# A two-layer image kernel: softplus arithmetic and part of the B-products move to GpSimd, and the state tiles shrink to one state

## The chip, the cores and the metric

The kernel runs on one core of one Trainium2 chip. The metric is the device time of one execution in microseconds: 26,680.71 us is the median of three runs before the change (26,676.87 to 26,696.96). The profile shows one further execution on the same core. Engines are named as in the profile: PE is the matrix engine, DVE the vector engine, ACT the activation engine, POOL is GpSimd, SP issues most of the transfers.

## The reference, cut to what matters

The input is an image batch of 4 x 128 x 128 x 128 floats. Layer 0 is a deformable convolution (a gather of sampled points, weighted and summed, with a residual). Layer 1 is a two-deep Mamba block over the rows of the picture: each row is a sequence of 128 steps with 256 inner channels and 16 states. The change touches layer 1 alone:

```python
def _selective_scan(u, delta, A, Bm, Cm, Dp):
    deltaA  = exp(einsum('btd,dn->btdn', delta, A))
    deltaBu = einsum('btd,btn->btdn', delta * u, Bm)
    def step(h, xs):
        dA, dBu, c = xs
        h = dA * h + dBu
        return h, einsum('bdn,bn->bd', h, c)
    ...
    return y + u * Dp

dt, Bm, Cm = split(u @ xw)
delta = softplus(dt @ dtw + dtb)
```

So each channel and each of 16 states needs a product of delta\*u with B, a recurrence along the sequence, and a product of its result with C, summed over the states.

## The kernel before

**Tiling.** Layer 1 is cut into blocks of SR = 4 rows of 128 points (TB = 512 points), with the 256 channels as NC = 2 halves of 128 partitions. One *job* is one block in one of the two Mamba layers. There are 32 blocks in a picture and 4 pictures, so 64 jobs for each picture and 256 in all. `jobs` takes two blocks at a time, so that two independent jobs alternate.

**What a job does.** `pre` makes u (convolution by matmul and Silu), the gate g, the rows of B and C (written to DRAM as `bcd`), and delta = softplus(pdt). Softplus is written as max(x,0) + ln(1+e^-|x|), with a correction e: ACT makes |x| (L538), e^-|x| (L539), w1 = 1+e (L545) and ln w1 (L546); DVE forms w1-1-e (L547), max(x,0) minus that (L548), the sum with the logarithm (L549) and du = delta\*u (L550). `main` then walks the 16 states in 8 steps of NQ = 2 states. In each step SP loads B and C broadcast to all partitions (L570), ACT writes zero into the first column of each sequence of `da` (L575, so that the recurrence begins anew there) and exp(delta\*A) into the rest (L580), and DVE makes hs = du\*B once per state (L586, 128x1024), the recurrence in place in `da` for both states at once (L592, 128x2048), and the product with C in place, both states at once (L596, 128x2048). PE sums the transposed result over the states in PSUM (L128). At the end DVE multiplies by the gate (L607), whose first operand is in PSUM.

**Order.** `layer1` calls `pre` for job i+1 before `main` for job i, so softplus of the next job is made while this job's states run. `layer1` of picture b is interleaved with `layer0` of picture b+1 by a loop that steps both. The pictures thus overlap: first layer 0 of picture 0 alone, then three pictures' worth of both layers together, then layer 1 of the last picture alone. In layer 0 every unit issues 8 indirect gathers from POOL (L364), which read their indices from SBUF, and multiplies what they brought with weights on DVE (L382). The order within an engine is set by a scheduler at build time[...].

**Buffers.** `da` has three fixed buffers of two states, `hs` has one buffer, B and C have two buffers each, `e` two half-width ones, `w1` one.

Of the kernel before, what the change touches and what calls it, by code (L numbers as in the profile page):

```python
# [10 lines left out]
F32 = mybir.dt.float32  # L11
# [52 lines left out]
def block_kernel(ctx: ExitStack, tc: tile.TileContext, a: dict, out: bass.AP):  # L64
# [68 lines left out]


    dw = loadw("dw", [P, NT, NT], pool=p2, tag="dbl")
    dwb = loadw("dwb", [P, NT], pool=p2, tag="ot")
    pw = loadw("pw", [P, NT, CG], pool=p2, tag="u")
    pwb = loadw("pwb", [P, 1], pool=p2, tag="w1")
    nc.vector.tensor_tensor(
# [15 lines left out]
    alog = loadw("alog", [P, NL, NC, NS], pool=p2, tag="dbl")  # L155
    nc.scalar.activation(aneg, alog, AF.Exp)
    nc.vector.tensor_scalar(aneg, aneg, -1.0, None, ALU.mult)
    dpar = loadw("dpar", [P, NL, NC], pool=p2, tag="ot")
    for l in range(NL):
        for c in range(NC):  # L160
            nc.vector.tensor_scalar(ddiag[:, l, c, :], ident, dpar[:, l, c : c + 1], None, ALU.mult)
    inw = loadw("inw", [P, NL, NC * P], a["inw"][:, :, 0 : NC * P], pool=p2, tag="yg")
    cvw = loadw("cvw", [P, NL, DCONV, NC * P], pool=p2, tag="hs")
    for l in range(NL):
        nc.vector.tensor_tensor(
            inc[:, l], cvw[:, l], inw[:, l].unsqueeze(1).to_broadcast([P, DCONV, NC * P]), ALU.mult
        )


# [289 lines left out]

    NDA = 3
    das = [cw.tile([P, NC, NQ, SR, P], F32, name=f"da{i}") for i in range(NDA)]
    zero = cw.tile([P, NC * NQ * SR], F32, name="zero")
    nc.vector.memset(zero, 0.0)
    n_da = [0]

    NH = 2
# [15 lines left out]
    def pre(st, l):  # L484

        blk = st["blk"]
        nm = f"{blk}_{l}"
        if l == 0:
            x1t = load_x1(blk, nm)
            st["h"] = next_h()  # L490
            scale, bias = gn2[blk * SR // H]
            nc.scalar.activation(
                st["h"][:, :, DCONV - 1 :], x1t.rearrange("p (s t) -> p s t", s=SR),
                AF.Identity, scale=scale, bias=bias,
            )
        h = st["h"]
        u = p2.tile([P, NC, TB], F32, tag="u", name=f"u_{nm}")
        for c in range(NC):
            px = ps1.tile([P, TB], F32, tag="t", name=f"pu_{nm}_{c}")
            for j in range(DCONV):  # L500
                nc.tensor.matmul(  # L501
                    px.rearrange("p (s t) -> p s t", s=SR),
                    inc[:, l, j, c * P : (c + 1) * P],
                    h[:, :, j : j + P],
                    start=(j == 0),
                    stop=(j == DCONV - 1),
                )
            nc.scalar.activation(u[:, c], px, AF.Silu, bias=cvb[:, l, c : c + 1])  # L508
        g = p2.tile([P, SR, NC * P], F32, tag="g", name=f"g_{nm}", bufs=2)
        for i in range(SR // 2):  # L510
            px = ps1.tile([P, 2, NC * P], F32, tag="t", name=f"pr_{nm}_{i}")
            for j in range(2):
                nc.tensor.matmul(
                    px[:, j], h[:, 2 * i + j, DCONV - 1 :], resw[:, l, :],
                    start=(j == 0), stop=True, skip_group_check=True,
                )

            tc.keep_in_program_order(nc.scalar.activation(g[:, 2 * i : 2 * i + 2], px, AF.Silu))
        pdb = ps1.tile([P, TB], F32, tag="t", name=f"pdb_{nm}")
        for c in range(NC):  # L520
            nc.tensor.matmul(pdb[0:XP], xpw[:, l, c, :], u[:, c], start=(c == 0), stop=(c == NC - 1))  # L521

        dbl = p2.tile([XP, TB], F32, tag="dbl", name=f"dbl_{nm}")
        nc.scalar.activation(dbl, pdb[0:XP], AF.Identity, bias=xpb)  # L524
        bcd = pd.tile([2 * NS, TB], F32, tag="bcd", name=f"bcd_{nm}")
        nc.sync.dma_start(bcd, dbl[DTR + 1 : XP, :])


        de = p2.tile([P, NC, TB], F32, tag="de", name=f"de_{nm}", bufs=2)
        du = p2.tile([P, NC, TB], F32, tag="du", name=f"du_{nm}", bufs=2)  # L530
        es, pdts = [], []
        for c in range(NC):
            pdt = ps1.tile([P, TB], F32, tag="t", name=f"pdt_{nm}_{c}")
            nc.tensor.matmul(
                pdt, dtw[:, l, c * P : (c + 1) * P], dbl[0 : DTR + 1, :], start=True, stop=True
            )
            e = p2.tile([P, TB], F32, tag="e", name=f"e_{nm}_{c}", bufs=2)
            nc.scalar.activation(e, pdt, AF.Abs)  # L538
            nc.scalar.activation(e, e, AF.Exp, scale=-1.0)  # L539
            es.append(e)  # L540
            pdts.append(pdt)
        for c in range(NC):
            e = es[c]
            w1 = p2.tile([P, TB], F32, tag="w1", name=f"w1_{nm}_{c}")
            nc.scalar.activation(w1, e, AF.Identity, bias=1.0)  # L545
            nc.scalar.activation(du[:, c], w1, AF.Ln)  # L546
            nc.vector.scalar_tensor_tensor(e, w1, 1.0, e, op0=ALU.subtract, op1=ALU.subtract)  # L547
            nc.vector.scalar_tensor_tensor(de[:, c], pdts[c], 0.0, e, op0=ALU.max, op1=ALU.subtract)  # L548
        nc.vector.tensor_tensor(de, de, du, ALU.add)  # L549
        nc.vector.tensor_tensor(du, de, u, ALU.mult)  # L550
        st.update(u=u, g=g, delta=de, du=du, bcd=bcd)

    def main(st, l):

        blk = st["blk"]
        nm = f"{blk}_{l}"

        y = psy.tile([P, SR, NC, P], F32, tag="y", name=f"y_{nm}")
        for i in range(SR):
            for c in range(NC):  # L560
# [1 line left out]
                    y[:, i, c], st["u"][:, c, i * P : (i + 1) * P], ddiag[:, l, c, :],  # L562
                    start=(i % 2 == 0 and c == 0), stop=False, skip_group_check=True,
                )
        for q in range(NS // NQ):
            bc = []
            for w in range(2):
                t = p2.tile([P, NQ, TB], F32, tag=f"bc{w}", name=f"bc{w}_{nm}_{q}", bufs=2)
                n0 = w * NS + q * NQ
                nc.sync.dma_start(t, st["bcd"][n0 : n0 + NQ, :].partition_broadcast(P))  # L570
                bc.append(t)
            da = das[n_da[0] % NDA]
            n_da[0] += 1

            nc.scalar.copy(da.rearrange("p c n s t -> p (c n s) t")[:, :, 0], zero)  # L575
            for c in range(NC):
                dv = st["delta"][:, c].rearrange("p (s t) -> p s t", s=SR)
                for n in range(NQ):
                    s = q * NQ + n
                    nc.scalar.activation(  # L580
                        da[:, c, n, :, 1:], dv[:, :, 1:], AF.Exp, scale=aneg[:, l, c, s : s + 1]
                    )
            hs = p2.tile([P, NC, NQ, TB], F32, tag="hs", name=f"hs_{nm}_{q}")

            for n in range(NQ):
                nc.vector.scalar_tensor_tensor(  # L586
                    hs[:, :, n, :], st["du"], ones[:, 0:1],
                    bc[0][:, n].unsqueeze(1).to_broadcast([P, NC, TB]),
                    op0=ALU.mult, op1=ALU.mult,
                )  # L590
            df = da.rearrange("p c n s t -> p (c n s t)")
            nc.vector.tensor_tensor_scan(  # L592
                df, df, hs.rearrange("p c n t -> p (c n t)"), zero[:, 0:1], ALU.mult, ALU.add
            )
            dc = da.rearrange("p c n s t -> p c (n s t)")
            nc.vector.scalar_tensor_tensor(  # L596
                dc, dc, ones[:, 0:1],
                bc[1].rearrange("p n t -> p (n t)").unsqueeze(1).to_broadcast([P, NC, NQ * TB]),
                op0=ALU.mult, op1=ALU.mult,
            )  # L600
            for c in range(NC):
                for n in range(NQ):
                    for i in range(SR):
                        add_transposed(y[:, i, c], da[:, c, n, i, :], False, q == NS // NQ - 1 and n == NQ - 1)
            yield
        gt = st["g"]
        nc.vector.tensor_tensor(gt, y.rearrange("p s c d -> p s (c d)"), gt, ALU.mult)  # L607
        yg = p2.tile([P, NC, TB], F32, tag="yg", name=f"yg_{nm}")
# [6 lines left out]
        if l < NL - 1:  # L615
            for c in range(NC):
                nc.tensor.matmul(po, ow[:, l, c, :], yg[:, c], start=(c == 0), stop=(c == NC - 1))
            st["h"] = next_h()
            nc.scalar.copy(st["h"][:, :, DCONV - 1 :], po.rearrange("p (s t) -> p s t", s=SR))
        else:  # L620
            x1t = load_x1(blk, f"o{nm}")
            for i in range(SR):
                o = po[:, i * P : (i + 1) * P]
                nc.tensor.matmul(o, x1t[:, i * P : (i + 1) * P], ident, start=True, stop=False)
                for c in range(NC):
                    nc.tensor.matmul(
                        o, yg[:, c, i * P : (i + 1) * P], ow[:, l, c, :], start=False, stop=(c == NC - 1)
                    )
            ot = p2.tile([P, SR, P], F32, tag="ot", name=f"ot_{nm}")
            nc.scalar.copy(ot.rearrange("p r c -> p (r c)"), po)  # L630
            b, row = divmod(blk * SR, H)
            nc.sync.dma_start(out[b, row : row + SR].rearrange("r w c -> w r c"), ot)
# [115 lines left out]
```

## Time and profile before

| | |
|---|---|
| median of 3 runs | 26,680.71 us |
| the profiled execution | 26,698.06 us |
| its span | 26,696.0 us |
| DVE busy | 23,505.8 us (88%), 14,042 instructions |
| PE busy | 19,620.5 us (73%) |
| POOL busy | 16,017.0 us (60%), 9,216 gathers |
| ACT busy | 11,605.1 us (43%) |
| first recurrence (L592) starts | 3,471.2 us |
| POOL's last gather starts | 21,045.0 us |
| mean granted clock of PE | 0.845 |

The profiled execution lies 17 us above the median, 2 us of it outside its span. The busy shares of the whole span are averages over three stages: until about 3,471 us there is only layer 0; until about 21,100 us both layers run together; after it only layer 1 of the last picture is left, and POOL has nothing to do. A group's row gives the busy time of all its instructions and the mean of one; instructions of DVE that follow each other overlap by about 0.08 us in the records, so start-to-start distances in the timeline are a little smaller than the durations.

### The profile page before, as it was taken

To read this page: it belongs to the slowest core of one execution; us is meant where nothing else is said; L and a number is where in the kernel's file an instruction comes from. 1 tells how busy PE (TensorE), PEld (TensorE's weight loads), DVE (VectorE), ACT (ScalarE), POOL (GpSimd) and SP (SyncE) were. 2 spreads that over 40 slices of the span, in tenths; PEclk is the share of its full clock that TensorE was granted. 3 is DMA by queue.
4 is the path that set the end of the run, shared out by engine and by line. 5 is a ranking of instruction groups with operands and counts; after the bars stand their busy time and mean duration, and the time that the engine had idled before them with its cause. 6 is when DMAs were issued, how large, how long until landed. Compare 5 with 4: busy or idle time off the path is not lost. (4 is left out here: it accounts for less than half of the span.)

```text
span 26696.0 us, 294801 instructions
## 1 busy us (share of the span) xinstructions
PE 19620.5 (73%) x112196; PEld 13523.4 (51%) x112196; DVE 23505.8 (88%) x14042; ACT 11605.1 (43%) x18181; POOL 16017.0 (60%) x9222
## 2 busy tenths in 40 slices
PE   4777788878888778887888778888888655555555
PEld 3444455555555555555555555555555443434344
DVE  2232289999999999999999999999999999999999
ACT  0000044444444544444444454444445455555554
POOL 4777777878877767888878667877878400000000
PEclk7888888888999888888998888899998866666666
DMA  5363344456544444455544444444444333333332
GB/s 146 114 172 107 106 147 155 157 170 183 165 153 154 149 144 155 158 173 181 164 154 153 148 143 151 156 150 152 154 154 156 130 107 106 107 106 107 107 106 102
DMA packets 1994602, 3804.53 MB, mean 143 GB/s; under 512 B 771796, under 2 KB 1116116, under 8 KB 1993053
## 3 DMA queue, kind: packets, MB, share of 16 engines
q1 hardware_dynamic: 1550812, 2577.13, 29.9%
q0 software_dynamic: 442368, 1208.55, 14.4%
q8 instruction: 880, 14.42, 0.2%
q14 instruction: 542, 4.43, 0.0%
HBM read 3567.63 MB, written 217.05 MB: 142 GB/s over the span
## 5 line engine op out<-in xcount | busy, mean ns | idle before, releaser
L364 POOL DMA_INDIRECT gt<-table,idx x9216 | 16016.3, 1738 | 5031.5 <-issue 2999.5
L592 DVE TENSOR_TENSOR_SCAN da<-da,zero,hs 128x2048 f32<-128x2048 f32 x2048 | 9176.1, 4481 | 351.7 <-ACT da L580 247.1
L128 PE MATMUL y<-ident,da 128*128 128x128 f32 x32768 | 5252.0, 326 | 3956.1 <-DVE da L596 3955.4
L580 ACT ACTIVATE da<-de,aneg 128x508 f32<-128x508 f32 x8192 | 5550.5, 712 | 5605.2 <-PE y L128 5351.0
L128 PEld LDWEIGHTS y<-ident,da 128*128 128x128 f32 x32768 | 4682.4, 171 | 4953.3 <-DVE da L596 2520.6
L415 PE MATMUL acc<-s,wc 128*64 128x256 f32 (+3 forms) x38400 | 6403.2, 453 | 761.4 <-ACT s L396 760.9
L586 DVE SCALAR_TENSOR_TENSOR hs<-du,ones,bc 128x1024 f32<-128x1024 f32 x4096 | 5093.2, 1277 | 0.0
L415 PEld LDWEIGHTS acc<-s,wc 128*64 128x64 f32 x38400 | 3352.0, 145 | 3083.2 <-issue 1446.2
L596 DVE SCALAR_TENSOR_TENSOR da<-da,ones,bc 128x2048 f32<-128x2048 f32 x2048 | 4807.9, 2348 | 25.9
L382 DVE TENSOR_TENSOR gw<-gt,wt 128x1024 f32<-128x1024 f32 x2304 | 2786.4, 1213 | 2133.3 <-DMA gt<-table,idx 1500.9
L128 PE MATMUL p<-ident,gw 128*128 128x128 f32 x18432 | 2724.3, 299 | 1714.1 <-DVE gw L382 1706.7
L128 PEld LDWEIGHTS p<-ident,gw 128*128 128x128 f32 x18432 | 2292.8, 154 | 2329.3 <-DVE gw L382 1752.7
L396 ACT COPY s<-p 128x512 f32<-128x512 f32 x1152 | 668.6, 581 | 3989.8 <-PE p L128 3982.0
L501 PE MATMUL pu<-hp,inc 128*128 128x512 f32 x4096 | 1808.3, 593 | 0.0
L580 ACT ACT_TABLE_LOAD x1016 | 1303.5, 1283 | 16.8 <-PE y L128 5.7
L501 PEld LDWEIGHTS pu<-hp,inc 128*128 128x128 f32 x4096 | 751.2, 188 | 865.9 <-issue 865.2
L508 ACT ACTIVATE u<-pu,w_cvb 128x512 f32<-128x512 f32 x512 | 324.6, 684 | 1468.9 <-PE y L561 1461.4
L561 PEld LDWEIGHTS y<-ddiag,u 128*128 128x128 f32 x4096 | 579.5, 200 | 192.0 <-issue 192.0
L612 PE MATMUL pyg<-ident,g 128*128 128x128 f32 x2048 | 353.9, 328 | 425.7 <-DVE g L607 424.8
L546 ACT ACT_TABLE_LOAD x500 | 641.5, 1283 | 8.9
L561 PE MATMUL y<-ddiag,u 128*128 128x128 f32 x4096 | 612.1, 284 | 0.0
L263 PE MATMUL pof<-xn,w_offw 128*64 128x512 f32 x2304 | 585.0, 613 | 20.0 <-ACT xn L257 12.0
(118 smaller groups left out, 11036.3 us busy)
## 6 DMA issues: line engine op xcount, KB each, us to landing
bc<-bcd SPq DMA_DIRECT2D x4096, 512.0 KB
gt<-table,idx POOLq DMA_INDIRECT x9216
table<-xt SPq DMA_DIRECT2D x984, 128.0 KB
xt<-in_x SPq DMA_DIRECT2D x124, 320.0 KB
xr<-in_x SPq DMA_DIRECT2D x128, 256.0 KB
x<-xo SPq DMA_DIRECT2D x128, 256.0 KB
x1t<-x SPq DMA_DIRECT2D x128, 256.0 KB
x1t_o<-x SPq DMA_DIRECT2D x128, 256.0 KB
```

What stands on the lines that cost most here:

```text
L128: nc.tensor.matmul(o, v, ident, is_transpose=True, start=start, stop=stop, skip_group_check=True)
L364: nc.gpsimd.indirect_dma_start(out=gt[:, v, r], out_offset=None, in_=flat, in_offset=bass.IndirectOffsetOnAxis(ap=idx[:, ri, o : o + 1], a ...
L382: nc.vector.tensor_tensor(gw.rearrange("p r s v c -> p (r s) v c"), gts[h].rearrange("p v r (s c) -> p (r s) v c", c=CG), wv.unsqueeze(3). ...
L396: nc.scalar.copy(st[:, :, 1 : W + 1], p4)
L415: nc.tensor.matmul(accs[b, j + i0][CG * g : CG * g + CG, q : q + rb - ra, :], wc[sl, v, e, :], st[p + 4 * g if p < 4 else 8][sl, ra:rb, kx ...
L501: nc.tensor.matmul(px.rearrange("p (s t) -> p s t", s=SR), inc[:, l, j, c * P : (c + 1) * P], h[:, :, j : j + P], start=(j == 0), stop=(j ...
L546: nc.scalar.activation(du[:, c], w1, AF.Ln)
L561: nc.tensor.matmul(y[:, i, c], st["u"][:, c, i * P : (i + 1) * P], ddiag[:, l, c, :], start=(i % 2 == 0 and c == 0), stop=False, skip_grou ...
L580: nc.scalar.activation(da[:, c, n, :, 1:], dv[:, :, 1:], AF.Exp, scale=aneg[:, l, c, s : s + 1])
L586: nc.vector.scalar_tensor_tensor(hs[:, :, n, :], st["du"], ones[:, 0:1], bc[0][:, n].unsqueeze(1).to_broadcast([P, NC, TB]), op0=ALU.mult, ...
L592: nc.vector.tensor_tensor_scan(df, df, hs.rearrange("p c n t -> p (c n t)"), zero[:, 0:1], ALU.mult, ALU.add)
L596: nc.vector.scalar_tensor_tensor(dc, dc, ones[:, 0:1], bc[1].rearrange("p n t -> p (n t)").unsqueeze(1).to_broadcast([P, NC, NQ * TB]), op ...
```

## The change

Four things change, all in layer 1, and some buffers with them.

1. *Softplus.* The four DVE instructions of softplus and delta\*u become four `tensor_tensor` instructions on POOL, each over 128x1024, and the fused forms are undone: ACT now also makes max(x,0) (a Relu from PSUM, one per half) and w1-1 (a second Identity). ACT's other softplus steps run on both halves at once where they read SBUF.
2. *Tiles of one state.* The loop runs over 16 states singly. `da` has four buffers of one state, whose first columns are zeroed once at the start; the recurrence writes into `hs` instead of into `da`, so the zero columns stay and ACT's copy of zeros (L575) is gone. The recurrence and the product with C become 128x1024 instructions, twice as many as before. The recurrence's initial value is the constant 0.0 instead of a one-element operand. `hs` has five buffers of one state.
3. *B-products.* In the last picture (`blk * SR // H == B - 1`) 12 of the 16 products with B, all but states 3, 7, 11 and 15, are POOL `tensor_tensor` instructions; in the other pictures all stay on DVE.
4. *Loads.* B is loaded for each state (three buffers), C for two states (two buffers): 24 loads in a job in place of 16, of the same bytes.

For room, the output tile `ot` takes the buffer of `w1`, and weights that are loaded at the start go through other buffers, one of them in two parts.

```diff
-    NDA = 3
-    das = [cw.tile([P, NC, NQ, SR, P], F32, name=f"da{i}") for i in range(NDA)]
-    zero = cw.tile([P, NC * NQ * SR], F32, name="zero")
-    nc.vector.memset(zero, 0.0)
+    NDA = 4
+    das = [cw.tile([P, NC, SR, P], F32, name=f"da{i}") for i in range(NDA)]
+    for t in das:
+        nc.vector.memset(t, 0.0)
...
+        e = p2.tile([P, NC, TB], F32, tag="e", name=f"e_{nm}")
+        w1 = p2.tile([P, NC, TB], F32, tag="w1", name=f"w1_{nm}")
         for c in range(NC):
...
-            e = p2.tile([P, TB], F32, tag="e", name=f"e_{nm}_{c}", bufs=2)
-            nc.scalar.activation(e, pdt, AF.Abs)
-            nc.scalar.activation(e, e, AF.Exp, scale=-1.0)
...
-            nc.scalar.activation(w1, e, AF.Identity, bias=1.0)
-            nc.scalar.activation(du[:, c], w1, AF.Ln)
-            nc.vector.scalar_tensor_tensor(e, w1, 1.0, e, op0=ALU.subtract, op1=ALU.subtract)
-            nc.vector.scalar_tensor_tensor(de[:, c], pdts[c], 0.0, e, op0=ALU.max, op1=ALU.subtract)
-        nc.vector.tensor_tensor(de, de, du, ALU.add)
-        nc.vector.tensor_tensor(du, de, u, ALU.mult)
+            nc.scalar.activation(e[:, c], pdt, AF.Abs)
+            nc.scalar.activation(de[:, c], pdt, AF.Relu)
+        nc.scalar.activation(e, e, AF.Exp, scale=-1.0)
+        nc.scalar.activation(w1, e, AF.Identity, bias=1.0)
+        nc.scalar.activation(du, w1, AF.Ln)
+        nc.scalar.activation(w1, w1, AF.Identity, bias=-1.0)
+
+        nc.gpsimd.tensor_tensor(e, w1, e, ALU.subtract)
+        nc.gpsimd.tensor_tensor(de, de, e, ALU.subtract)
+        nc.gpsimd.tensor_tensor(de, de, du, ALU.add)
+        nc.gpsimd.tensor_tensor(du, de, u, ALU.mult)
...
+        on_pool = set(range(NS)) - {3, 7, 11, 15} if blk * SR // H == B - 1 else set()
...
-        for q in range(NS // NQ):
...
-            nc.scalar.copy(da.rearrange("p c n s t -> p (c n s) t")[:, :, 0], zero)
...
+        for n in range(NS):
+            bs = p2.tile([P, TB], F32, tag="bs", name=f"bs_{nm}_{n}", bufs=3)
+            nc.sync.dma_start(bs, st["bcd"][n : n + 1, :].partition_broadcast(P))
+            if n % NQ == 0:
+                cs = p2.tile([P, NQ, TB], F32, tag="cs", name=f"cs_{nm}_{n}", bufs=2)
+                nc.sync.dma_start(cs, st["bcd"][NS + n : NS + n + NQ, :].partition_broadcast(P))
...
+            hs = p2.tile([P, NC, TB], F32, tag="hs", name=f"hs_{nm}_{n}", bufs=5)
...
+            if n in on_pool:
+                nc.gpsimd.tensor_tensor(hs, st["du"], bv, ALU.mult)
+            else:
+                nc.vector.scalar_tensor_tensor(hs, st["du"], ones[:, 0:1], bv, op0=ALU.mult, op1=ALU.mult)
...
             nc.vector.tensor_tensor_scan(
-                df, df, hs.rearrange("p c n t -> p (c n t)"), zero[:, 0:1], ALU.mult, ALU.add
+                hf, da.rearrange("p c s t -> p (c s t)"), hf, 0.0, ALU.mult, ALU.add
             )
...
+            nc.vector.scalar_tensor_tensor(hs, hs, ones[:, 0:1], cv, op0=ALU.mult, op1=ALU.mult)
...
-            ot = p2.tile([P, SR, P], F32, tag="ot", name=f"ot_{nm}")
+            ot = p2.tile([P, NC, TB], F32, tag="w1", name=f"ot_{nm}")[:, 0].rearrange("p (r c) -> p r c", r=SR)
```

## The prediction

> **What bounds the kernel now.** I read the page's slices first, then the stretches by stage, then the group rows, then the timeline of DVE and POOL.
>
> ```profile
> DVE  2232289999999999999999999999999999999999
> ...
> POOL 4777777878877767888878667877878400000000
> ```
>
> The digits are tenths of each fortieth of the span. Once layer 1 runs, DVE is full to the end; POOL is well used until the last picture and then idle. By stage (columns: window, length, PE, PEld, DVE, ACT, POOL busy with counts, PE clock, DMA share, GB/s):
>
> ```profile
> 8000.00:14000.00 6000.00, 4802.57 (x28217) 3309.21 (x28219) 5873.27 (x3522) 2901.32 (x4573) 4599.66 (x2320) 0.89 0.50 159
> 14000.00:20000.00 6000.00, 4797.07 (x28207) 3297.84 (x28204) 5846.47 (x3439) 2910.15 (x4589) 4562.25 (x2329) 0.89 0.46 151
> 21300.00:26696.00 5396.00, 2810.47 (x12755) 2157.37 (x12753) 5114.30 (x2515) 2721.11 (x4141) 0.00 (x0) 0.69 0.31 106
> ```
>
> DVE is busy 98% in the overlapped stage and 95% in the last picture; PE (80%), ACT (48%) and DMA have room. DVE's work per job is the time per job. The rows that make it up:
>
> ```profile
> L592 DVE TENSOR_TENSOR_SCAN da<-da,zero,hs 128x2048 f32<-128x2048 f32 x2048 | 9176.1, 4481 | 351.7 <-ACT da L580 247.1
> L586 DVE SCALAR_TENSOR_TENSOR hs<-du,ones,bc 128x1024 f32<-128x1024 f32 x4096 | 5093.2, 1277 | 0.0
> L596 DVE SCALAR_TENSOR_TENSOR da<-da,ones,bc 128x2048 f32<-128x2048 f32 x2048 | 4807.9, 2348 | 25.9
> ```
>
> From the first recurrence (3,471 us) to 21,300 us lie 192 jobs, 92.9 us each. The window after holds 517 recurrences, 64.6 jobs, 83.5 us each.
>
> The view that decides is the timeline of both engines at one place of the overlapped stage (start, duration, engine, line):
>
> ```profile
> 12006.12 0.81 DVE L215 TENSOR_TENSOR xt<-xt,row_s 128x640 f32<-128x640 f32 x1
> 12006.85 4.47 DVE L592 TENSOR_TENSOR_SCAN da<-da,zero,hs 128x2048 f32<-128x2048 f32 x1
> 12011.25 0.80 DVE L216 TENSOR_TENSOR xt<-xt,row_b 128x640 f32<-128x640 f32 x1
> ```
>
> ```profile
> 12006.18 1.57 POOL L364 DMA_INDIRECT gt<-table,idx  x1 [0.30 <-issue]
> 12008.06 4.03 POOL L364 DMA_INDIRECT gt<-table,idx  x1 [0.31 <-issue]
> ```
>
> A gather that starts inside L215 ends 0.82 us after L215's end (12007.75 against 12006.93); the next starts 1.2 us into the recurrence and ends 0.77 us after its end (12012.09 against 12011.32). An undisturbed gather lasts 0.95 us. So POOL's read of the index stands still until DVE's instruction is over. It does not beside a DVE instruction that has one operand in PSUM:
>
> ```profile
> 3942.94 1.23 DVE L607 TENSOR_TENSOR g<-y,g 128x1024 f32<-128x1024 f32 x1 [2.18 <-PE y L128]
> ```
>
> ```profile
> 3943.24 0.95 POOL L364 DMA_INDIRECT gt<-table,idx  x1 [0.30 <-issue]
> ```
>
> **What the Trainium skill says.** "SBUF — State Buffer", section Who interferes with whom: a DVE instruction with two SBUF inputs and a GpSimd instruction that reads SBUF exclude each other over a shared read interface, and whichever comes second waits for the whole of the first. This trace agrees for POOL behind DVE (the lines above); DVE behind POOL it can't show, because POOL's only reads are one index per partition. "GPSIMD Engine Reference", section Elementwise — side-by-side cycle accounting: a `tensor_tensor` over 2048 floats takes 4,497 ns on GpSimd, with about 2.5 cycles per element at 1.2 GHz as floor. No POOL `tensor_tensor` is in this trace, so that is my price: half of it, 2.25 us for 128x1024, an estimate.
>
> **The change, part by part.** All sums are per job, then times 192 (overlapped jobs) and 64 (last picture).
>
> *Tiles of one state.* In the last picture one step of two states takes 9.40 us from one L596 start to the next (23,006.02 to 23,015.42): 2.27 for L596, 2.61 for two L586, 4.52 for L592. Start to start, an STT costs 1.20 us for 1024 elements (two L586 last 2.48, one 1.28) and 2.27 for 2048, thus 0.13 fixed. A recurrence followed by work that does not need it costs 4.40 (23,020.29 to 23,024.69), so half of it costs (4.40-0.13)/2+0.13 = 2.27. The built order puts two states side by side (B, B, scan, scan, C, C), which removes the small waits on the instruction just before: 2 x (1.20+2.27+1.20) = 9.34 us. I take no change; the range holds 0.1 us per step, 0.2 ms in all. ACT loses L575 (427.9 us), which nothing waited for.
>
> *Softplus off DVE.* L547 to L550 are 347.0+349.0+311.3+309.3 = 1,316.6 us, 5.14 per job; less six overlaps of 0.08, DVE gains 4.7 us per job.
>
> *B-products off DVE, last picture.* 12 x 1.20 = 14.4 us per job.
>
> *POOL's share.* 4 instructions per overlapped job, 16 per job of the last picture. Every large DVE instruction of layer 1 except L607 has two SBUF inputs, and so has L382, so DVE is inside such an instruction nearly always. I take exclusion to work both ways: each POOL instruction gets its turn at the end of a DVE instruction, as the gathers do, and DVE stands still for h = 2.25 us. Then, against the present jobs:
> overlapped: -4.7 + 4 x 2.25 = +4.3 us, x 192 = +0.83 ms;
> last picture: DVE's own work is 16 x 2.27 + 16 x 1.20 + 4 x 1.20 + 1.1 = 61.4 us, plus 16 x 2.25 = 36.0, is 97.4 us against 83.5 (of which 2.5 was idle): +13.9 us, x 64 = +0.89 ms.
> Sum +1.72 ms. In general the change is 1792 h - 2.3 ms (h in us, product in us): break-even at h = 1.29 us. Bounds on h: 2.13 by the page's floor, 1.7 if only the streaming part (two reads per element) excludes, 2.5 with a hand-over of 0.1 us each way: +0.7 to +2.2 ms.
>
> *Work on ACT.* Two Relus (0.59 each, as L538) and one more Identity come in, one table load of 1.28 us and the L575 copies go; ACT stays near 45 us a job of over 90. `w1` now also waits for the output transfer of `ot`: nothing if ACT has its present slack, up to 3 us in 128 jobs, 0.4 ms, if the exponentials are late.
>
> *POOL as a queue.* In the overlapped stage POOL is occupied 4,599.66 of 6,000 us plus about 670 us of gaps between its gathers, 88%, or 82 us of a job. Four instructions with their turn-waits of about 1 us add 13: 95 us against a DVE job of 97. The gathers stand behind these four, which stand behind ACT's chain; L382 on DVE waits for the gathers. I count nothing, since shorter DVE instructions let gathers through more often; if it fails, some 5 us a job, 1 ms.
>
> *Loads.* Same bytes, 8 more issues of 0.32 us on SP per job; with the DMA share at 0.3 to 0.5, hidden.
>
> Profiled execution 26,698 + 1,720 = 28,418; the median lies 17 below: 28,400 us.
>
> **The rivals.**
> *Exclusion as above* (68%): 28,400, own range 27,400 to 29,300. For it: the waits above end with DVE's instruction whatever its length. Against: only one direction is seen.
> *POOL streams beside DVE* (16%), the other side: if DVE does not stand still for POOL, the last picture drops to 61.4+2.5 = 64 us a job (-1.25 ms), and the overlapped job falls until POOL's queue binds, 82 + 4 x 2.35 = 91 us (-0.35 ms): about 25,100. It decides from h below 1.29 us. Against it: a wait that lasts a whole instruction looks like a lock, and a lock that only one side honours would be strange.
> *Half a hold* (10%): POOL holds the interface only in pieces or half the time, h near 1.1: -0.35 ms, 26,350.
> *Exclusion, and POOL's queue binds too* (6%): late gathers stall L382: about 29,500.
>
> **How the numbers follow.** The likeliest case gives 28,400. To leave out no more than 20%, the range must hold nearly all of the first case, the third and half of the fourth: 26,000 to 29,600. Within 0.2% (about 53 us, what a measurement can tell) lies only a sliver of the third case. Faster: 16% + 6% of the third; slower: 68% + 6% + 2%; rounded 0.22, 0.03, 0.75.
>
> **What would show it.** Under exclusion, POOL's `tensor_tensor` last 2.3 us and more, DVE's recurrences and STTs have longer means than 2.35 and 1.28 us in the last picture (DVE busy although its work shrank), and that picture's jobs take about 97 us. If DVE keeps 2.35 and 1.28 and the last picture's jobs take 64 us, I am wrong on the direction. If L382 or L364 show long waits on POOL's new lines, the fourth case holds. A POOL instruction far from 2.25 us moves the sum by 1.8 ms per microsecond.

## The result, and the profile after

The changed kernel takes 28,118.73 us (median of 4 runs, 28,114.72 to 28,125.8), against 26,678.79 us for the kernel before (26,671.07 to 26,696.96): the ratio is 1.0539, with a 95% interval from 1.0521 to 1.0557. That is 1,440 us slower, where 1,720 us were forecast (28,400 us in all, with a range from 26,000 to 29,600). The profiled execution took 28,121.26 us, its span 28,119.4.

The page's slices after the change:

```profile
DVE  2232299999999999999999999999999999999999
...
POOL 4777777788878577788878587888886555555555
```

DVE is as full as it was, in the last picture too, although 12 of its 16 products with B and the four softplus steps are gone from there. POOL now works to the end. The two stages, in the same columns as before:

```profile
8000.00:14000.00 6000.00, 4614.72 (x27224) 3228.24 (x27222) 5943.45 (x4035) 2620.91 (x3754) 4692.02 (x2483) 0.87 0.50 154
```

```profile
22500.00:27500.00 5000.00, 2370.72 (x10269) 1716.95 (x10270) 4673.77 (x1920) 2053.41 (x2824) 2915.29 (x829) 0.65 0.28 92
```

In the second row 1,920 instructions of DVE take 4,674 us, 2.4 us each, in a stage where most of them cover 1,024 elements per partition. The groups of the page say which have grown:

```profile
L589 DVE TENSOR_TENSOR_SCAN hs<-da,hs 128x1024 f32<-128x1024 f32 x4096 | 10443.0, 2580 | 408.3 <-POOL hs L585 389.1
...
L592 DVE SCALAR_TENSOR_TENSOR hs<-hs,ones,cs 128x1024 f32<-128x1024 f32 x4096 | 6415.8, 1595 | 3.5
L587 DVE SCALAR_TENSOR_TENSOR hs<-du,ones,bs 128x1024 f32<-128x1024 f32 x3328 | 4781.6, 1463 | 51.8 <-PE y L128 45.8
...
L585 POOL TENSOR_TENSOR hs<-du,bs 128x1024 f32<-128x1024 f32 x768 | 2702.7, 3532 | 2559.2 <-PE y L128 1981.1
```

The product with C had 1.2 us of work before and now has a mean of 1,595 ns over the whole run. In the last picture alone, the groups of that stretch give 2,176 ns for it and 3,101 ns for the recurrence:

```profile
L589 DVE TENSOR_TENSOR_SCAN hs<-da,hs 128x1024 f32<-128x1024 f32 x831 | 2545.2, 3101 | 326.3 <-POOL hs L585 321.0
L592 DVE SCALAR_TENSOR_TENSOR hs<-hs,ones,cs 128x1024 f32<-128x1024 f32 x830 | 1774.1, 2176 | 0.0
```

These are means over two kinds of instruction, those with a POOL instruction in their way and those without. The timeline of one spot in the last picture separates them (start, duration, engine, line; neighbours of one line are put together as x2):

```profile
24038.35 3.37 DVE L587 SCALAR_TENSOR_TENSOR hs<-du,ones,bs 128x1024 f32<-128x1024 f32 x1
24040.71 3.20 POOL L547 TENSOR_TENSOR de<-de,e 128x1024 f32<-128x1024 f32 x1
24041.81 8.53 DVE L589 TENSOR_TENSOR_SCAN hs<-da,hs 128x1024 f32<-128x1024 f32 x2
24043.87 4.33 POOL L585 TENSOR_TENSOR hs<-du,bs 128x1024 f32<-128x1024 f32 x1
```

```profile
24068.99 4.46 DVE L589 TENSOR_TENSOR_SCAN hs<-da,hs 128x1024 f32<-128x1024 f32 x2
```

Two recurrences without a POOL instruction take 4.46 us. The pair at 24,041.81 takes 8.53 us, 4.07 more, and two POOL instructions run in it. They run in turns. POOL's L547 is issued while DVE is inside L587 and ends at 24,043.91, 2.19 us after L587's end. Then comes the first recurrence. L585, issued at 24,043.87, has to wait for it, so it lasts 4.33 us, and the second recurrence waits for L585 in its turn. DVE's loss is about 2 us for each POOL instruction.

For all that follows, the time of one job is read from the starts of the recurrences: from the first of job 0 to the first of job 192, over 192 (*overlapped*), and from there to the end of the span, over 64 (*last picture*).

| kernel | overlapped, us/job | last picture, us/job |
|---|---|---|
| before | 93.13 | 83.51 |
| after | 96.16 | 96.42 |

The difference is 3.03 x 192 + 12.91 x 64 = 1,408 us; the spans differ by 1,423, the rest being the first recurrence, which starts 15 us later.

### The profile page after: what moved, and what is told of

Same layout as the page of the kernel before. It is cut to its first block, busy times and chain, and to the rows that moved or that the text cites. A ratio compares the mean times of both kernels' runs of the same rounds, so it can differ in the third digit from the quotient of the medians.

```text
span 28119.4 us, 300192 instructions
## 1 busy us (share of the span) xinstructions
PE 19666.9 (70%) x112196; PEld 13560.6 (48%) x112196; DVE 25039.4 (89%) x15837; ACT 10879.9 (39%) x15509; POOL 20480.8 (73%) x11014
## 3 DMA queue, kind: packets, MB, share of 16 engines
q0 software_dynamic: 442368, 1208.55, 14.4%
## 4 chain that ended last, share of the span: by engine, by line
issue 33%; POOL 33%; DVE 23%; DMA 5%; PE 4%; ACT 2%; SPq 1%; DVEq 0%; POOLq 0%; ACTq 0%
POOL gt L365 27%; DVE hs L589 8%; DVE hs L592 7%; DVE hs L587 5%; DMA gt<-table,idx 4%; DVE gw L383 2%; POOL hs L585 2%; POOL de L548 1%; POOL de L547 1%; POOL e L546 1%; PE acc L416 1%; PE pdb L522 1%; POOL du L549 1%; PE y L128 1%; SPq L232 0%
## 5 line engine op out<-in xcount | busy, mean ns | idle before, releaser
L365 POOL DMA_INDIRECT gt<-table,idx x9216 | 14372.2, 1559 | 4524.1 <-issue 2862.5
L589 DVE TENSOR_TENSOR_SCAN hs<-da,hs 128x1024 f32<-128x1024 f32 x4096 | 10443.0, 2580 | 408.3 <-POOL hs L585 389.1
L128 PE MATMUL y<-ident,hs 128*128 128x128 f32 x32768 | 5337.2, 326 | 5464.9 <-DVE hs L592 5454.3
L128 PEld LDWEIGHTS y<-ident,hs 128*128 128x128 f32 x32768 | 4618.9, 170 | 6593.8 <-DVE hs L592 5975.4
L592 DVE SCALAR_TENSOR_TENSOR hs<-hs,ones,cs 128x1024 f32<-128x1024 f32 x4096 | 6415.8, 1595 | 3.5
L587 DVE SCALAR_TENSOR_TENSOR hs<-du,ones,bs 128x1024 f32<-128x1024 f32 x3328 | 4781.6, 1463 | 51.8 <-PE y L128 45.8
L585 POOL TENSOR_TENSOR hs<-du,bs 128x1024 f32<-128x1024 f32 x768 | 2702.7, 3532 | 2559.2 <-PE y L128 1981.1
L128 PE MATMUL p<-ident,gw 128*128 128x128 f32 x18432 | 2674.8, 299 | 1189.0 <-DVE gw L383 1182.3
L128 PEld LDWEIGHTS p<-ident,gw 128*128 128x128 f32 x18432 | 2345.0, 156 | 1613.9 <-DVE gw L383 1146.5
L502 PE MATMUL pu<-hp,inc 128*128 128x512 f32 x4096 | 1809.3, 593 | 12.6 <-ACT hp L611 12.6
L502 PEld LDWEIGHTS pu<-hp,inc 128*128 128x128 f32 x4096 | 751.0, 188 | 881.6 <-issue 862.7
L548 POOL TENSOR_TENSOR de<-de,du 128x1024 f32<-128x1024 f32 x256 | 914.6, 3573 | 11.8
L549 POOL TENSOR_TENSOR du<-de,u 128x1024 f32<-128x1024 f32 x256 | 854.3, 3337 | 15.9
L547 POOL TENSOR_TENSOR de<-de,e 128x1024 f32<-128x1024 f32 x256 | 828.9, 3238 | 17.1
```

The source lines that it names most:

```text
L128: nc.tensor.matmul(o, v, ident, is_transpose=True, start=start, stop=stop, skip_group_check=True)
L365: nc.gpsimd.indirect_dma_start(out=gt[:, v, r], out_offset=None, in_=flat, in_offset=bass.IndirectOffsetOnAxis(ap=idx[:, ri, o : o + 1], a ...
L502: nc.tensor.matmul(px.rearrange("p (s t) -> p s t", s=SR), inc[:, l, j, c * P : (c + 1) * P], h[:, :, j : j + P], start=(j == 0), stop=(j ...
L548: nc.gpsimd.tensor_tensor(de, de, du, ALU.add)
L549: nc.gpsimd.tensor_tensor(du, de, u, ALU.mult)
L585: nc.gpsimd.tensor_tensor(hs, st["du"], bv, ALU.mult)
```

## The experiments

Ten kernels were run. The runs e3, e5, e6 and e8, and later e9 and e10, were on two other chips, where the first stage of these kernels, with layer 0 alone, lasts some 0.6 ms longer (the kernel before takes 27,331.57 and 27,355.62 us there). They are therefore compared by the ratio to the kernel before on the same chip, and by the time of a job, which is the same on all chips where nothing differs: the overlapped job takes 92.65 us in e1 and 92.71, 92.72 and 92.66 in e3, e5 and e9.

| run | what it is | ratio to before [95%] | overlapped | last picture |
|---|---|---|---|---|
| e1 | tiles of one state alone | 0.988 [0.9864, 0.9897] | 92.65 | 79.94 |
| e2 | e1 + softplus on POOL | 1.0205 [1.0188, 1.0222] | 96.12 | 82.87 |
| e3 | e1 + B-products on POOL | 1.0123 [1.0106, 1.014] | 92.71 | 90.02 |
| after | e1 + both | 1.0539 [1.0521, 1.0557] | 96.16 | 96.42 |
| e4 | e1 + 12 unused POOL products | 1.0456 [1.0438, 1.0473] | 92.66 | 103.92 |
| e5 | e1 + 12 unused POOL memsets | 0.9872 [0.9856, 0.9889] | 92.72 | 79.48 |
| e6 | e1 + 12 unused POOL copies | 1.0101 [1.0084, 1.0118] | 92.74 | 89.10 |
| e7 | after, other 12 products on POOL | 1.0487 [1.047, 1.0505] | 96.17 | 94.65 |
| e8 | e1, plain `tensor_tensor` everywhere | 1.0023 [1.0013, 1.0032] | 94.89 | 78.63 |
| e9 | e1, plain `tensor_tensor` in the last picture | 0.9865 [0.9849, 0.9882] | 92.66 | 78.58 |
| e10 | e1, recurrence with a one-element operand | 0.9995 [0.9986, 1.0004] | 93.70 | 81.40 |

**e1: the tiles of one state alone.** Against the kernel after, softplus is back on DVE in the form of before, and no product is on POOL; ACT makes softplus as before, and `ot` has its own buffer again:

```diff
-        nc.gpsimd.tensor_tensor(e, w1, e, ALU.subtract)
-        nc.gpsimd.tensor_tensor(de, de, e, ALU.subtract)
-        nc.gpsimd.tensor_tensor(de, de, du, ALU.add)
-        nc.gpsimd.tensor_tensor(du, de, u, ALU.mult)
...
+            nc.vector.scalar_tensor_tensor(e, w1, 1.0, e, op0=ALU.subtract, op1=ALU.subtract)
+            nc.vector.scalar_tensor_tensor(de[:, c], pdts[c], 0.0, e, op0=ALU.max, op1=ALU.subtract)
+        nc.vector.tensor_tensor(de, de, du, ALU.add)
+        nc.vector.tensor_tensor(du, de, u, ALU.mult)
...
-        on_pool = set(range(NS)) - {3, 7, 11, 15} if blk * SR // H == B - 1 else set()
+        on_pool = set()
```

> Only the tiles of one state: softplus and all B-products are back on DVE. Theory 1 (DVE stands still while a POOL instruction reads SBUF, and that alone made the kernel slower): a step of two states is 9.34 us against 9.40 before, so 26,550 to 26,750 us, the same as before within 0.3%. Theory 2 (the smaller tiles cost the time: twice the recurrences and C-products, more loads): most of the 1,440 us stays, 27,500 us or more.

Measured: 26,386.45 us where the kernel before takes 26,705.62 on the same chip, ratio 0.988, thus 319 us faster. This missed what was expected (26,550 to 26,750 us). The timeline of DVE in the last picture shows what a step of two states was, from one product with C to the next in the kernel before,

```profile
23006.02 2.35 DVE L596 SCALAR_TENSOR_TENSOR da<-da,ones,bc 128x2048 f32<-128x2048 f32 x1
...
23015.42 2.35 DVE L596 SCALAR_TENSOR_TENSOR da<-da,ones,bc 128x2048 f32<-128x2048 f32 x1
```

and what it is in e1:

```profile
23002.02 4.49 DVE L591 TENSOR_TENSOR_SCAN hs<-da,hs 128x1024 f32<-128x1024 f32 x2
23006.40 2.48 DVE L594 SCALAR_TENSOR_TENSOR hs<-hs,ones,cs 128x1024 f32<-128x1024 f32 x2
23008.78 2.50 DVE L589 SCALAR_TENSOR_TENSOR hs<-du,ones,bs 128x1024 f32<-128x1024 f32 x2
23011.17 4.49 DVE L591 TENSOR_TENSOR_SCAN hs<-da,hs 128x1024 f32<-128x1024 f32 x2
```

From one pair of recurrences to the next it is 9.15 us for two states, where the kernel before needs 9.40. Why it is shorter is taken up in e10. The gain of the other parts of the change thus has to be counted from here, not from before.

**e2: softplus on POOL, without the B-products.** Against after:

```diff
-        on_pool = set(range(NS)) - {3, 7, 11, 15} if blk * SR // H == B - 1 else set()
+        on_pool = set()
```

> The changed kernel with every B-product on DVE; only softplus is on POOL. Theory 1 with a hold of 2.1 us: against the tiles alone +3.7 us in each of 192 overlapped jobs and +1 to +3.7 us in each of 64 of the last picture, 750 to 950 us more than the tiles alone, about 27,450 us. Theory 2 (POOL's work runs beside DVE): 0.9 ms less than the tiles alone.

Measured: ratio 1.0205, 868 us more than e1, inside the 750 to 950 us expected. Against e1 the overlapped job is 3.47 us longer although DVE has 4.7 us less to do (six instructions, since two of the four lines run once for each half), so the four POOL instructions cost DVE (3.47 + 4.7) / 4 = 2.04 us each. In ratios, softplus on POOL is worth +3.25% and the B-products, from e2 to after, +3.34%.

**e3: the B-products on POOL, with softplus on DVE.** This is the kernel after with softplus back on DVE as in e1; the line shown for e2 stays as it is in after.

> The tiles alone plus the 12 B-products per job of the last picture on POOL; softplus stays on DVE. Theory 1 with the hold that the first runs gave, 2.05 us: each moved product costs 2.05 and saves 1.20, so +10 us per job, 64 jobs, 650 us more than the tiles alone (26,386), about 27,040 us, 26,950 to 27,150. Theory 3 (waiting for results is what costs): close to the tiles alone or less, 26,400 us or below, since POOL's chain for softplus, on which the first product of a job waited, is gone.

Measured: ratio 1.0123; the last picture's job is 10.08 us longer than in e1, although DVE has 12 x 1.20 us less to do: 10.08 / 12 + 1.20 = 2.04 us for each POOL product, as expected. Of this 0.2 us is no stand-still behind POOL's reads but a wait of DVE for POOL's result (147.9 us over 63 jobs, 2.3 us per job).

**e4: products that nobody needs.** The runs so far leave a second reading open: that DVE doesn't stand still for POOL's reads but is late because it needs POOL's results. Here DVE does all its products as in e1, and POOL makes the 12 products in addition, into a tile that nothing reads:

```diff
             if n in on_pool:
-                nc.gpsimd.tensor_tensor(hs, st["du"], bv, ALU.mult)
-            else:
-                nc.vector.scalar_tensor_tensor(hs, st["du"], ones[:, 0:1], bv, op0=ALU.mult, op1=ALU.mult)
+                dummy = pb.tile([P, NC, TB], F32, tag="gw", name=f"dummy_{nm}_{n}", bufs=2)
+                nc.gpsimd.tensor_tensor(dummy, st["du"], bv, ALU.mult)
+            nc.vector.scalar_tensor_tensor(hs, st["du"], ones[:, 0:1], bv, op0=ALU.mult, op1=ALU.mult)
```

> The tiles alone, with DVE doing all of its work itself; in the last picture POOL makes 12 products with B in each job as well, into a tile that nobody reads. The extra products are work the reference does not have. Theory 1: DVE stands still for them although nothing waits for their results: 64 x 12 x 2.1 us = 1.6 ms, less up to 0.16 ms that fall into DVE's idle time, so 1,400 to 1,600 us more than the tiles alone, with recurrences of up to 4.4 us. Theory 3 (DVE lost time only because it had to wait for POOL's results, not at the port): no change against the tiles alone, within 60 us.

Measured: ratio 1.0456; the last picture's job grows by 23.98 us, 2.00 us for each unused product. The timeline of the last picture:

```profile
24004.82 1.27 DVE L594 SCALAR_TENSOR_TENSOR hs<-hs,ones,cs 128x1024 f32<-128x1024 f32 x1
24006.01 2.28 DVE L591 TENSOR_TENSOR_SCAN hs<-da,hs 128x1024 f32<-128x1024 f32 x1
24008.21 1.26 DVE L589 SCALAR_TENSOR_TENSOR hs<-du,ones,bs 128x1024 f32<-128x1024 f32 x1
24008.48 3.19 POOL L588 TENSOR_TENSOR dummy<-du,bs 128x1024 f32<-128x1024 f32 x1 [4.67 <-DMA bs<-bcd]
24009.39 3.36 DVE L594 SCALAR_TENSOR_TENSOR hs<-hs,ones,cs 128x1024 f32<-128x1024 f32 x1
```

POOL's product is issued at 24,008.48 inside L589, and ends at 24,011.67, 2.20 us after L589 has ended. The next DVE instruction lasts 3.36 us in place of the 1.27 of the same line one step earlier. No wait is recorded before it, and nothing in it depends on POOL. Nor is the loss a wait elsewhere: from 22,500 to 27,500 us DVE is busy for 4,999 of the 5,000 us, so it is DVE's instructions themselves that have become longer, by 24.8 us per job, of which 0.8 us fills what was idle time in e1. The growth over e1 is 1,534 us, inside the 1,400 to 1,600 expected. This settles the direction that the profile before could not show: DVE stands still behind POOL as POOL does behind DVE.

**e5 and e6: a memset and a copy in place of the unused product.** They tell apart what of a POOL instruction holds DVE up. In e5 a one-element copy by ACT goes ahead of each memset, so that they are spread over the job.

```diff
-                nc.gpsimd.tensor_tensor(dummy, st["du"], bv, ALU.mult)
+                nc.scalar.copy(dummy[:, 0, 0:1], da[:, 0, 0, 1:2])
+                nc.gpsimd.memset(dummy, 0.0)
```

> As the unused products, but POOL writes zeros (128x1024, no SBUF input) 12 times in each job of the last picture; the zeros go to a tile that nobody reads, and ACT writes one column of it before each so that they stay in their place. Theory 1 in the form that the reads exclude each other: no change against the tiles alone, 26,330 to 26,450 us. Theory 1 in the wider form that any POOL access to SBUF stops DVE: 64 x 12 x about 0.9 us = 0.7 ms more, 27,000 us or above.

```diff
-                nc.gpsimd.tensor_tensor(dummy, st["du"], bv, ALU.mult)
+                nc.gpsimd.tensor_copy(dummy, st["du"])
```

> As the unused products, but POOL copies delta*u (one SBUF input, 128x1024) 12 times in each job of the last picture into a tile that nobody reads. Theory 1: DVE stands still for as long as POOL reads, with one input about half as long as with two, 0.9 to 1.1 us: 64 x 12 x 1.0 = 0.77 ms more than the tiles alone, 27,050 to 27,250 us. If only two-input POOL instructions exclude DVE: 26,386 us, no change.

Measured: the memsets cost nothing (ratio 0.9872, e1 0.988); the copies cost (89.10 - 79.94) / 12 = 0.76 us each, less than the 0.9 to 1.1 us that were expected. In e5's timeline two memsets last 0.95 us beside products with C that keep their 2.49 us for two:

```profile
24010.83 0.95 POOL L589 MEMSET dummy<- 128x1024 f32 x1 [8.20 <-ACT dummy L588]
24011.39 2.49 DVE L595 SCALAR_TENSOR_TENSOR hs<-hs,ones,cs 128x1024 f32<-128x1024 f32 x2
24013.01 0.95 POOL L589 MEMSET dummy<- 128x1024 f32 x1 [1.23 <-ACT dummy L588]
```

In e6's, two recurrences beside POOL's copies take 6.09 us, 1.60 more than the 4.49 of e1:

```profile
23995.41 6.09 DVE L591 TENSOR_TENSOR_SCAN hs<-da,hs 128x1024 f32<-128x1024 f32 x2
23996.33 19.86 POOL L588 COPY dummy<-du 128x1024 f32<-128x1024 f32 x8
```

So the cost goes with the reads: none, one and two inputs cost 0, 0.76 and 2.0 us. A copy costs less than half of what a product costs, and why it is not half was not looked into. That writes are free agrees with the Trainium skill, page "SBUF — State Buffer", section Who interferes with whom, which says that a DVE instruction with two SBUF inputs does not contend with a GpSimd instruction that only writes.

**e7: the lateness of some of POOL's products.** In the kernel after, DVE waits for POOL a few states into each job of the last picture. From the timeline:

```profile
24097.67 4.66 POOL L585 TENSOR_TENSOR hs<-du,bs 128x1024 f32<-128x1024 f32 x2 [13.26 <-PE y L128]
24100.05 8.70 DVE L589 TENSOR_TENSOR_SCAN hs<-da,hs 128x1024 f32<-128x1024 f32 x2 [5.42 <-POOL hs L585]
```

and from the waits of that stretch (us in total, times, longest):

```profile
DVE hs L589 <- POOL hs L585: 321.0, 52, 7.5
```

POOL waits for an `hs` buffer, and a buffer comes free when PE has added its state to the sum (L128). PE adds up the states of a job in one PSUM tile, so it can't take up a new job before DVE's gate has read the old sums; here the gate (L599) ended at 24,083.37. But PE then does other work first, the most of it the convolution of the next job (L502), and begins on the new job's states only 13.2 us after the gate:

```profile
24088.96 7.08 PE L502 MATMUL pu<-hp,inc 128*128 128x512 f32 x16
...
24096.55 2.24 PE L128 MATMUL y<-ident,hs 128*128 128x128 f32 x19
```

Until then no `hs` buffer is free, and POOL can't begin (13.26 us in the line above, ended by PE). This is read from the timeline; no run moved the convolution. In e7 the first four products of a job are DVE's, and POOL has the other 12:

```diff
-        on_pool = set(range(NS)) - {3, 7, 11, 15} if blk * SR // H == B - 1 else set()
+        on_pool = set(range(4, NS)) if blk * SR // H == B - 1 else set()
```

> The changed kernel with another choice of the 12 states that POOL makes in the last picture: 4 to 15 instead of all but 3, 7, 11 and 15, so DVE has its own work at the start of a job, where it now waits 6 us for POOL's first product. Theory 1: the wait goes, but what POOL did during it now holds up DVE: 1 to 4 us per job, 60 to 250 us less than the changed kernel's 28,119. Theory 3 (waiting for results is the cost): at least 6 us x 64 = 380 us less, 27,740 us or below.

Measured: 28,005.77 us, ratio 1.0487. The wait is gone; the only entry left in the list of DVE's waits there is

```profile
DVE g L599 <- PE y L128: 57.8, 45, 1.4
```

but the job is only 1.77 us shorter, of 6 us of wait. In after, the first of the two products shown above lies wholly in DVE's wait and costs DVE nothing more (the two take 4.66 us, so 2.33 each for POOL undisturbed); the second already holds up the recurrence that begins at 24,100.05, and the pair of recurrences takes 8.70 us. Without the wait more of POOL's work takes its turn with DVE's: DVE's instructions take 90.1 us per job in after and 93.6 in e7. So more than half of the wait comes back as longer instructions, and removing it is worth 113 us of the 1,440, as expected (60 to 250).

**e8: no operand of one element in the products.** The products with B and C go through `scalar_tensor_tensor` with a column of ones; a plain `tensor_tensor` computes the same.

```diff
-                nc.vector.scalar_tensor_tensor(hs, st["du"], ones[:, 0:1], bv, op0=ALU.mult, op1=ALU.mult)
+                nc.vector.tensor_tensor(hs, st["du"], bv, ALU.mult)
...
-            nc.vector.scalar_tensor_tensor(hs, hs, ones[:, 0:1], cv, op0=ALU.mult, op1=ALU.mult)
+            nc.vector.tensor_tensor(hs, hs, cv, ALU.mult)
```

> The tiles alone with both products on DVE as plain tensor_tensor instead of scalar_tensor_tensor with a column of ones. In the traces a tensor_tensor costs 1.135 us start to start and the other form 1.196. If DVE's own time is the bound: 8,192 x 0.06 us = 0.5 ms less, 25,850 to 25,950 us. If the gathers of the overlapped stage need the head of the other form, in which they got through, to read their indices: the last picture gains 0.12 ms and the overlapped stage nothing or less, 26,250 us or above.

Measured: ratio 1.0023 where e1 has 0.988. The gain that was expected shows only in the last picture (78.63 against 79.94 us per job); the overlapped job is 2.24 us longer. The groups of POOL between 8,000 and 20,000 us, first in e1, then in e8:

```profile
L365 POOL DMA_INDIRECT gt<-table,idx x4675 | 8031.8, 1718 | 3965.5 <-DVE gw L383 2533.0 <-issue 1260.8 <-DVE loc L289 84.7
```

```profile
L365 POOL DMA_INDIRECT gt<-table,idx x4546 | 9897.1, 2177 | 2106.4 <-issue 1289.0 <-DVE gw L383 740.2 <-DMA gt<-table,idx 28.1
```

A gather takes 2,177 ns in place of 1,718, and DVE now waits for what it brings; the group of DVE's multiplication with the weights, e1 and e8:

```profile
L383 DVE TENSOR_TENSOR gw<-gt,wt 128x1024 f32<-128x1024 f32 x1167 | 1391.0, 1214 | 23.3 <-PE p L128 22.5
```

```profile
L383 DVE TENSOR_TENSOR gw<-gt,wt 128x1024 f32<-128x1024 f32 x1138 | 1364.5, 1218 | 541.5 <-DMA gt<-table,idx 499.3 <-PE p L128 22.1 <-issue 15.7
```

So the plain form saves DVE some 60 ns per product (1,214 and 1,217 ns against 1,272 and 1,284 in the same window), and the gathers beside it get longer. That they lose a chance to read their index is the expectation's reading; the runs show only the longer gathers. The idle time, 541.5 - 23.3 us over some 126 jobs, is 4.1 us per job, of which the shorter products give about half back.

**e9: the plain form in the last picture alone**, where no gather runs.

```diff
+            alone = blk * SR // H == B - 1
+            if alone:
+                nc.vector.tensor_tensor(hs, st["du"], bv, ALU.mult)
...
+            if alone:
+                nc.vector.tensor_tensor(hs, hs, cv, ALU.mult)
```

> The tiles alone, with the products as plain tensor_tensor in the last picture only, where there are no gathers. From the run with tensor_tensor everywhere: 1.3 us per job of the last picture and nothing elsewhere, 85 us less than the tiles alone; as a ratio to the kernel before 0.985 against 0.988. If tensor_tensor hurts for another reason than the gathers: no gain, 0.988 or above.

Measured: ratio 0.9865; the job of the last picture is 1.36 us shorter than in e1, 87 us in 64 jobs, where 85 were expected. The interval overlaps that of e1 (both are wider than the difference), so the gain is read from the job time and not shown by the total. Of the versions without work that nobody needs, e1 and e9 beat both kernels, by 1.2% and 1.35% against before.

**e10: what in the tiles of one state made e1 faster.** The recurrence's initial value is again an operand of one element, as it was before the change:

```diff
-                hf, da.rearrange("p c s t -> p (c s t)"), hf, 0.0, ALU.mult, ALU.add
+                hf, da.rearrange("p c s t -> p (c s t)"), hf, zero[:, 0:1], ALU.mult, ALU.add
```

> The tiles alone, with the recurrence's initial value again a one-element operand instead of the constant 0.0. If that operand is what made two recurrences of the tiles alone cheaper than one of double length was (4.38 us against 4.40, where 4.54 was worked out): 4,096 x 0.07 us = 0.29 ms more, ratio to the kernel before about 0.998. If the gain of the tiles alone comes from their order and from ACT's lost zeros: no change, ratio 0.988.

Measured: ratio 0.9995 [0.9986, 1.0004], higher than the 0.998 or so that was expected. The recurrence's group on the pages of e1 and e10:

```profile
L591 DVE TENSOR_TENSOR_SCAN hs<-da,hs 128x1024 f32<-128x1024 f32 x4096 | 9248.7, 2283 | 6.5 <-DVE hs L589 0.5
```

```profile
L593 DVE TENSOR_TENSOR_SCAN hs<-da,zero,hs 128x1024 f32<-128x1024 f32 x4096 | 9505.6, 2342 | 6.3
```

The constant is worth 59 ns per recurrence by the records, and by the job times (93.70 - 92.65) x 192 + (81.40 - 79.94) x 64 = 295 us, which is nearly the whole gain of e1. What is left of the smaller tiles cancels: with the operand, the overlapped job is 0.57 us longer than before and that of the last picture 2.1 us shorter. Two effects of similar size stand behind this. Two instructions over 1,024 elements take longer than one over 2,048 (2 x 2,342 ns against 4,481 for the recurrence), so DVE's busy time per job grows against before, by 1.8 us (overlapped) and 0.9 (last picture); and its idle time shrinks by 1.2 and 3.0 us. Most of the idle time that goes in the last picture is the recurrence's wait for ACT's `da`: the recurrence's row of before, which the prediction shows, has 351.7 us of idle time, 247.1 of it ended by ACT, and the row above has 6.3. Whether this wait went because of the fourth `da` buffer, the smaller tiles, the order or the missing copies of zeros was not separated.

## Why the prediction came out as it did

**What bounds the kernel, and in which direction it moves: right.** DVE is the bound in both stages, and DVE and POOL exclude each other both ways (e4). The case that forecast a faster kernel, POOL streaming beside DVE, would have left e4 at the time of e1, and the last picture at 64 us per job; it took 96.42, where 97.4 were worked out. The signs that it named came: POOL's products have a mean of 3,532 ns, and DVE's recurrences and products in the last picture have grown.

The terms of the sum, predicted and measured, in ms:

| term | predicted | measured | from |
|---|---|---|---|
| softplus, overlapped jobs | +0.83 | +0.67 | e2 - e1, 3.47 x 192 |
| softplus, last picture | +0.28 | +0.19 | e2 - e1, 2.93 x 64 |
| B-products, last picture | +0.81 | +0.87 | after - e2, 13.55 x 64 |
| tiles, overlapped jobs | 0 | -0.09 | e1 - before, 0.48 x 192 |
| tiles and idle time, last picture | -0.19 | -0.23 | e1 - before, 3.57 x 64 |
| sum | +1.73 | +1.41 | |

**The hold h: mis-sized.** The prediction took 2.25 us, half of the price that the Trainium skill gives in "GPSIMD Engine Reference", section Elementwise — side-by-side cycle accounting. As a price for POOL's own duration it is near (2.33 us undisturbed). But the time for which it holds DVE up is less: 2.00 us (e4; 2.07 with the idle time that the holds fill) and 2.04 (e2). About 0.3 us of each POOL instruction lies beside DVE's work. At 1,792 instructions, 0.2 us less is 0.36 ms less; this is the largest error. The bound of 2.13 us that the prediction took from the page's floor is therefore no lower bound of the hold. (It rests on about 2.5 cycles per element, which the page gives in its section Instruction dispatch; the section that the prediction names gives about 2.6.) The break-even that the prediction gave, 1.29 us, is well below what was measured. For a single product the rule is plainer: moving it takes 1.20 us from DVE and gives it 2.0 to stand still.

**The tiles of one state: "no change" was wrong.** The two-state step of e1 is 9.15 us, where the prediction reckoned 9.34 and took no change from 9.40, and the total moved by -0.32 ms where the range for it was 0.2. The working took every duration from the recurrence of before, which has the one-element operand, and did not price that the change replaces it by a constant: 295 us (e10). Of the idle time it dropped a part in the last picture without giving a reason (83.5 against 61.4 + 4.7 + 14.4 = 80.5 us, the -0.19 ms of the table; 3.0 us, where it names 2.5, and its own window shows 5,396 - 5,114 us over 64.6 jobs, 4.4 us). That the recurrence waits for ACT's `da` stands in the row that it shows, and it made nothing of it. For the last picture the error is small, but the mechanism is not the one reckoned: the constant was not in the sum. (Its 92.9 us per overlapped job is 93.1, since the stretch up to 21,300 us holds 191.4 jobs; the sum does not use it.)

**A wait that was not foreseen: POOL's products a few states into a job.** The prediction reckoned the last picture's job as DVE's own work plus 16 full holds, 61.4 + 36.0 us, without idle time. In fact DVE stands idle there for 6.3 us per job, nearly all of it waiting for POOL, which waits for PE to free an `hs` buffer (e7). DVE's instructions take 90.1 us per job; those of e1, less the products and softplus, take 79.1 - 14.4 - 4.7 = 60.0. So the holds make 30.1 us, 1.9 for each of the 16 POOL instructions, since a product in DVE's wait costs nothing. That 97.4 us came so near to 96.42 is thus luck: 6.3 us of idle time that were left out stand against 5.9 us of holds and 1.4 us of DVE's own work too many. It is also why the B-products look well predicted. What removing the wait is worth by itself is less, 113 us (e7).

**POOL's queue and the loads: rightly counted at nothing.** In the overlapped stage of after DVE's multiplication with the weights stood idle for 16.2 us of 12,000 and not for a gather; the 541.5 us of e8 show what the case of late gathers would have looked like. The reason that the prediction gave, that shorter DVE instructions let gathers through more often, fits: the mean gather between 8,000 and 20,000 us went from 1,971 ns before to 1,737 after. ACT's extra work and the additional loads left no gap either: DVE is busy 11,886 us of these 12,000, in e1 11,867.

## What to carry to other kernels

Where two engines keep each other from reading, as DVE and POOL do here, moving work from the busy one to the other is paid in the time for which the moved instruction holds the busy one up. Compare this hold with the instruction removed (2.0 us against 1.20 here) before asking whether there is idle time on the other engine. If only a probe can tell, give the idle engine work that nobody reads, as in e4, and look at the busy engine's durations. And price the form of an instruction, down to a constant in place of an operand of one element, when it runs thousands of times on the engine that is the bound.

## What the runs showed of the hardware

- A POOL `tensor_tensor` of 128x1024 floats lasts 2.33 us undisturbed and holds up a DVE instruction with two SBUF inputs for 2.0 us. A copy of the same size costs DVE 0.76 us, a memset nothing.
- The turns are taken instruction by instruction: the second of two POOL instructions waits for one whole recurrence, and the second recurrence for it.
- An operand of one element as initial value costs the recurrence 59 ns (e1, e10). A product in the form with a column of ones lasts some 60 ns longer than the plain one (e1, e8); 1.36 us per job of 32 products, or about 40 ns each, reaches the time of a job (e1, e9). Here the whole form differs, not the operand alone.
- The slower forms let POOL's gathers through sooner: the mean gather between 8,000 and 20,000 us takes 1,428 ns with the operand on recurrence and products (e10), 1,718 with it on the products alone (e1), 2,177 with it on neither (e8). In the kernel before, with the operand on both but recurrences of twice the length, it takes 1,971. That there is a gap at the head of such an instruction is the likeliest reason, and was not shown by itself.
